# Expert jobs that write the finished token rows: one change to a graph layer with a mixture of experts

## The chip, the core and the metric

The kernel runs on one core of a Trainium2 chip. The metric is the device time of one execution in microseconds (us), taken without the profiler; the median of three runs of the kernel before is 1281.22 us (1278.25 to 1282.19). A core has five engines that matter here, each with its own instruction stream run in order: PE (TensorE, matrix products), DVE (VectorE, elementwise work), ACT (ScalarE), POOL (GpSimd; here it issues the indirect transfers), and SP (SyncE; here it issues the plain transfers). They wait for one another through semaphores.

## The reference

Two layers on 6,250 nodes of 256 numbers, with 100,000 edges sorted by destination:

```
x = x + gnn(layernorm(x), edges)      # attention over incoming edges, 4 heads of 64
x = x + ffn(layernorm(x))             # one of 8 experts for each node ("token")
```

The graph layer gathers, for each edge, two projections of its source node, mixes them by the edge's two factors, and sums them at the destination with softmax weights. In the expert layer each token goes to the expert with the highest gate probability:

```
idx   = argmax(probs);  prb = max(probs)
buf   = zeros(E, C, D).at[idx, pos].set(x)         # x is normalized here
ybuf  = relu(buf @ w1 + b1) @ w2 + b2              # 256 -> 1024 -> 256
y_tok = ybuf[idx, pos] * prb                       # and then added to the token's x2
```

Below, h is the normalized token, x2 the token before it (input plus graph layer), and prob its probability. The result of a token is y * prob + x2.

## The kernel before, in words

Preparation (the first 70 us) normalizes all nodes, projects them into a table in DRAM (`node_tab`), and turns the edge lists.

**Edge phase.** The edges come in 66 blocks of twelve tiles of 128 edges (`order`), from the highest destination down. For a block b, `gathers(b)` (L1045) issues on POOL one indirect transfer for each tile, into one of three buffers `gt`, three blocks ahead. `messages(b)` (L1053 on, DVE) mixes the rows, `places(b)` makes the one-hot matrix `hot`, `products(b)` the weighted messages `v`, and `windows(b, half)` sums them on PE (L1140); finished sums go from ACT to DRAM by SP (L1151). The main loop (L1505) writes this order out by hand; every engine's stream follows it, with `step_routing` and `step_experts` between the parts.

**Routing.** When the sums of a chunk of four token tiles are complete, `route` (L1161) loads them, forms x2 and h next to each other in one row `hx` of 514 numbers (h, x2, token number + 1, prob), picks the expert and the slot, and queues an indirect store of each tile's rows on POOL (`put`, L1259) into a buffer `bufs[p]` in DRAM. It also stores x2 alone in `x2_d` (L1190), except in the last pass.

**Passes.** Tokens are taken in four passes (LASTS, PASS): pass p gives each expert 256, 384, 256 and 128 slots. The slots are more than the tokens, so `bufs` are cleared first (`clear`, L922, from a tile of zeros; `clear_last`), a few clears in each of the early blocks. A pass's experts can start when all its tokens are put.

**Expert jobs.** `experts` (L1385) is a generator that yields after each piece with a cost; `step_experts` runs pieces up to a budget (SHARE) a block from block 13 on, so that PE has them between the edge sums. A job is one expert in one pass: `fetch_rows` (L1311) loads its slots, `columns` transposes h, then two products with `w1t` (L1409) and `w2t` (L1426), both loaded a job or two ahead on SP. `outputs` (L1341) comes one piece later: it adds the bias on DVE (L1346) and stores y to `ybufs[p]`. In the last pass `last_outputs` instead forms y * prob + x2 with `weighted` (L1372) from the row's second half, and `write_last` scatters the result to `out` from POOL.

**The last part.** After the edge loop (L1549) the edge buffers are given up for a third set of expert weights. While the remaining jobs run, `fetch_and_finish` (L1455) works off the tokens of the first three passes in pairs of tiles: `fetch_outputs` gathers their y from `ybufs` by an indirect transfer on POOL and loads x2 from `x2_d` on SP (L1446); `finish`, three pairs later, forms y * prob + x2 on DVE (`weighted`, L1374) and stores it to `out` on SP (L659). 22 pairs and 8 jobs of 128 slots are done this way. `weighted` also sums each row into a column of `finite`, by which a last check decides whether a slow general path has to run.

Of the kernel before, what the change touches and what calls it, by code (L numbers as in the profile page):

```python
# [8 lines left out]
F32 = mybir.dt.float32  # L9
# [5 lines left out]
P = 128  # L15
# [504 lines left out]
def kernel(  # L520
# [28 lines left out]
    nc = tc.nc  # L549
    N, D = x.shape  # L550
    NE = src.shape[0]
    _, H, O = attn.shape
    E, _, FF = w1.shape
# [5 lines left out]
    NT = -(-N // P)  # L559
# [32 lines left out]
    NP = len(PASS)  # L592
    SM = max(PASS)
    SLOTS = [E * S for S in PASS]
# [8 lines left out]
    dram = ctx.enter_context(tc.tile_pool(name="dram", bufs=1, space=bass.MemoryType.DRAM))  # L603
    node_tab = dram.tile([N, ROW], F32, name="node_tab")
    sums = dram.tile([TROWS, ACC], F32, name="sums")
    x2_d = dram.tile([NT * P, D], F32, name="x2_d")

    BW = 2 * D + 2

    bufs = [dram.tile([n + NT * P, BW], F32, name=f"buf{p}") for p, n in enumerate(SLOTS)]  # L610
# [3 lines left out]
    const = fast.enter_context(tc.tile_pool(name="const", bufs=1))  # L614
# [16 lines left out]
    nc.vector.memset(ones, 1.0)  # L631
    eps_t = const.tile([P, 1], F32, name="eps_t")
    nc.vector.memset(eps_t, EPS)
    zeros = const.tile([P, 1024], F32, name="zeros")
    nc.vector.memset(zeros, 0.0)

    no_edge = const.tile([P, 1], F32, name="no_edge")
# [28 lines left out]
    def moments(pool, t, k):  # L666

        st = pool.tile([P, k, nc.vector.BN_STATS_DIM], F32, name="ln_st")
        mv = pool.tile([P, k, nc.vector.BN_AGGR_DIM], F32, name="ln_mv")
        for n in range(k):  # L670
            nc.vector.bn_stats(st[:, n, :], t[:, n, :])
            nc.vector.bn_aggr(mv[:, n, :], st[:, n, :])
        sd = pool.tile([P, k], F32, name="ln_sd")
        nc.scalar.activation(sd, mv[:, :, 1], AF.Sqrt, bias=eps_t)
        return mv, sd
# [24 lines left out]
    with tc.tile_pool(name="p1", bufs=2) as p1, \  # L700
# [191 lines left out]
        for c in range(len(parts)):  # L892
# [8 lines left out]
            for n0 in range(0, len(parts[c]), 2):  # L901
                k = min(2, len(parts[c]) - n0)
# [18 lines left out]

    def clear(p, r):  # L922

        nc.sync.dma_start(bufs[p][r:r + 512, 0:D].rearrange("(p n) d -> p n d", n=4),
                          zeros.rearrange("p (n d) -> p n d", n=4))

    def clear_last():

        J = SLOTS[NP - 1] // P
        for j in range(0, J, 2):  # L930
            nc.sync.dma_start(bufs[NP - 1][j * P:(j + 2) * P, D:BW].rearrange("(p n) k -> p n k", n=2),
                              zeros[:, 0:2 * (D + 2)].rearrange("p (n k) -> p n k", k=D + 2))

    clears = [(p, r) for p in range(NP) for r in range(0, SLOTS[p], 512)]


    nc.sync.dma_start(sums[N:TROWS, :], zeros[0:TROWS - N, 0:ACC])
# [45 lines left out]
    prob = ep.tile([P, NT], F32, name="prob")  # L983
# [13 lines left out]
    with tc.tile_pool(name="p4", bufs=1) as p4, tc.tile_pool(name="p5", bufs=2) as p5, \  # L997
# [163 lines left out]
        def route(c, p):  # L1161


            tiles = chunks[c]
            k, n0 = len(tiles), tiles[0]
            n1, r0 = n0 + k, n0 * P
            hx = p4.tile([P, CK, BW], F32, name="hx", bufs=2)[:, :k, :]
            h, x2 = hx[:, :, 0:D], hx[:, :, D:2 * D]
# [17 lines left out]
            attn_out = part[:, :, 0:H * O].rearrange("p n (h o) -> p n h o", h=H)  # L1186
            nc.vector.tensor_mul(attn_out, attn_out, den.unsqueeze(3).to_broadcast([P, k, H, O]))
            nc.vector.tensor_add(x2, x2, part[:, :, 0:H * O])
            if p < NP - 1:
                nc.sync.dma_start(x2_d[r0:r0 + k * P, :].rearrange("(n p) d -> p n d", p=P), x2)  # L1190
            mv, sd = moments(p4, x2, k)
            yield 0.0
            normalized(p4, h, x2, mv, sd, k)
# [91 lines left out]
        w1s, w2s, xs, xm = {}, {}, {}, {}  # L1285
# [25 lines left out]
        def fetch_rows(i):  # L1311

            if i == taken["fetched"] and i < len(jobs) and jobs[i][0] < taken["rows"]:
                taken["fetched"] = i + 1
                p, e = jobs[i]
                S = PASS[p]
                J = S // P
                xs[i] = p5.tile([P, SM // P, D], F32, name="xe", bufs=3)[:, :J, :]
                rows = bufs[p][e * S:(e + 1) * S, :].rearrange("(p j) d -> p j d", j=J)
                nc.sync.dma_start(xs[i], rows[:, :, 0:D])  # L1320
                if p == NP - 1:
                    xm[i] = p6.tile([P, J, D + 2], F32, name="xm", bufs=E)
                    nc.sync.dma_start(xm[i], rows[:, :, D:BW])

# [16 lines left out]
        def outputs(py, i, j0, k):  # L1341
            p, e = jobs[i]
            S = PASS[p]
            J = S // P
            y = p5.tile([P, 2, D], F32, name="y")[:, :k, :]
            nc.vector.tensor_add(y, py, b2b[:, e, :].unsqueeze(1).to_broadcast([P, k, D]))  # L1346
            if p < NP - 1:
                nc.sync.dma_start(
                    ybufs[p][e * S:(e + 1) * S, :].rearrange("(p j) d -> p j d", j=J)[:, j0:j0 + k, :], y)
            else:  # L1350
                scatters.append((last_outputs(y, xm[i], e), xm[i]))
            if e == E - 1 and j0 + k == J and p < NP - 1:
                tiles = list(range(LASTS[p], LASTS[p - 1] if p else NT))
                due.extend((p, tiles[i:i + 2]) for i in range(0, len(tiles), 2))

        scatters, due = [], []
        finite = p4.tile([P, NT + SLOTS[NP - 1] // P], F32, name="finite")
        nc.vector.memset(finite, 0.0)

        def last_outputs(y, xe, e):  # L1360

            J = PASS[NP - 1] // P
            number, pr = xe[:, :, D], xe[:, :, D + 1]
            to = p6.tile([P, J], F32, name="to_f")
            nc.vector.tensor_scalar(to, number, 0.0, float(2 * N), op0=OP.is_equal, op1=OP.mult)
            row = p6.tile([P, J], I32, name="row_l", bufs=E)
            nc.vector.scalar_tensor_tensor(row, number, -1.0, to, op0=OP.add, op1=OP.add)
            for j in range(J):
                weighted(xe[:, j, 0:D], y[:, j, :], pr[:, j:j + 1], xe[:, j, 0:D], NT + e * J + j)
            return row  # L1370

        def weighted(to, y, w, x2, k):  # L1372

            nc.vector.scalar_tensor_tensor(to, y, w, x2, op0=OP.mult, op1=OP.add, accum_out=finite[:, k:k + 1])  # L1374
# [10 lines left out]
        def experts():  # L1385
# [6 lines left out]
            for i, (p, e) in enumerate(jobs):  # L1392
# [6 lines left out]
                for q in (i, i + 1):  # L1399
                    fetch_rows(q)  # L1400
# [33 lines left out]
        fetched = []  # L1434

        def fetch_outputs():

            p, tiles = due.pop(0)
            k, n0 = len(tiles), tiles[0]
            yg = p6.tile([P, 2, D], F32, name="yg", bufs=6)[:, :k, :]  # L1440
            for n in range(k):
                nc.gpsimd.indirect_dma_start(  # L1442
                    out=yg[:, n, :], out_offset=None, in_=ybufs[p],
                    in_offset=bass.IndirectOffsetOnAxis(ap=to_get[:, n0 + n:n0 + n + 1], axis=0))
            xr = p6.tile([P, 2, D], F32, name="xr", bufs=4)[:, :k, :]
            nc.sync.dma_start(xr, x2_d[n0 * P:(n0 + k) * P, :].rearrange("(n p) d -> p n d", p=P))  # L1446
            fetched.append((tiles, yg, xr))

        def finish():
            tiles, yg, xr = fetched.pop(0)  # L1450
            for n, t in enumerate(tiles):
                weighted(yg[:, n, :], yg[:, n, :], prob[:, t:t + 1], xr[:, n, :], t)
            store_nodes(out, yg, tiles)

        def fetch_and_finish(lag):  # L1455
# [47 lines left out]
        for b in range(3):  # L1503
            gathers(b)
        for b in range(NB + 1):  # L1505
            for clear_at in clears[2 * b - 2:2 * b] if b else ():
                clear(*clear_at)
            if b == E + 1:
                clear_last()
            if b < NB:  # L1510
                messages(b)
            step_routing()
            if b == NB - 2:

                last_chunk = routes_of(next_c)
                next_c += 1
                assert next_p == NP - 1
                next(last_chunk)
            if b == NB:
                routing.append(last_chunk)  # L1520
            if b:
                windows(b - 1, 0)
            step_experts(SHARE / 2)
            step_routing()
            if b < NB:
                places(b)
            step_routing()
            if b < NB:
                products(b)
            step_routing()  # L1530
            if b:
                windows(b - 1, 1)
            taken["released"] = taken["rows"]
            step_experts(SHARE / 2)
            while next_c < len(chunks) - 1 and done_at[next_c] < b:
                routing.append(routes_of(next_c))
                next_c += 1
            step_routing()
            pool_work.extend(todo)
            del todo[:]  # L1540
            if b + 3 < NB:
                gathers(b + 3)
            if wait_pass and not pool_work:
                taken["rows"] = wait_pass.pop() + 1
                i = (taken["rows"] - 1) * E
                if taken["jobs"] >= i - 1:
                    fetch_rows(i)
                    fetch_rows(i + 1)
        edge_pools.close()  # L1549
        p6 = last_pools.enter_context(tc.tile_pool(name="p6", bufs=2))  # L1550
# [102 lines left out]
```

## Time and profile before

| | |
|---|---|
| median of three runs | 1281.22 us |
| the profiled execution | 1762.93 us, span 1761.1 us |
| clock granted to PE in it, mean | 0.788 |
| POOL: edge gathers (L1045) | 782, 951 ns each |
| POOL: token gathers (L1442) | 44, 966 ns each |
| DVE: weighted sums (L1374) | 44 on tokens, 480 ns each; 8 in the last pass |
| SP: x2 stored (L1190), loaded (L1446) | 11 of 512 KB, 22 of 256 KB |
| SP: clears | 16 of 512 KB, 4 of 258 KB |
| SP: rows of a job (L1320) | 16 of 256 KB, 8 of 384 KB, 8 of 128 KB |
| bytes moved | 218.47 MB |

The profiled execution is much longer than the runs: it holds long stretches in which several engines stand still together. A line of groups gives line, engine, operation, tiles and count, then busy us and mean ns of one, then the idle time before them and what ended it. In order of time, a line is start, duration, engine and line, and in brackets the wait before it. Lines of waits give the total, the number and the longest, in us. "issue" is time in which the engine waited for nothing that the profile shows; "remote" or "an unknown queue" is a wait whose releaser the profile doesn't have.

### The profile page before, as it was taken

How to read it: one execution, taken by the hardware profiler on the slowest of the kernel's cores; microseconds unless marked ns; L12 is line 12 of the kernel's file. 1: busy time of each engine (PE TensorE's matmuls, PEld its weight loads, DVE VectorE, ACT ScalarE, POOL GpSimd, SP SyncE). 2: the span in 40 equal slices, each digit the busy share in tenths (PEclk: the TensorE clock that was granted, in tenths of full speed). 3: DMA queues.
4: the chain of work that ended last, by engine and by line, in shares of the span. 5: the costliest groups of instructions: out<-in, count | busy, mean ns of one | idle time of the engine just before them, and what ended most of it. 6: DMA issues, size and time to landing. Idle time of an engine off the chain costs nothing.

```text
span 1761.1 us, 14755 instructions
## 1 busy us (share of the span) xinstructions
PE 1110.9 (63%) x4658; PEld 893.4 (51%) x4658; DVE 870.6 (49%) x1879; ACT 282.0 (16%) x754; POOL 863.6 (49%) x912
## 2 busy tenths in 40 slices
PE   5531532544685656856577586476874787779875
PEld 5520422433574545745356365354653566568765
DVE  7652534756674544626247345543752446455322
ACT  3300100111220202112012111110201111111321
POOL 2577357256666162553653562734564563630443
PEclk9765767667887777868687796778886898879998
DMA  8233433345453434433443351433432344333893
GB/s 255 80 86 83 118 87 100 92 128 156 140 154 102 123 106 127 128 103 102 115 128 98 98 144 44 113 92 104 124 89 69 104 123 136 103 109 122 307 366 105
DMA packets 154149, 218.47 MB, mean 124 GB/s; under 512 B 20198, under 2 KB 125963, under 8 KB 153933
## 3 DMA queue, kind: packets, MB, share of 16 engines
q1 hardware_dynamic: 121981, 142.51, 25.4%
q0 software_dynamic: 31440, 73.83, 16.6%
q10 hardware_dynamic: 640, 1.09, 0.2%
q8 instruction: 39, 0.64, 0.2%
q14 instruction: 49, 0.40, 0.1%
HBM read 160.50 MB, written 57.25 MB: 124 GB/s over the span
## 4 chain that ended last, share of the span: by engine, by line
PE 41%; DVE 18%; another core or an unknown queue 17%; issue 15%; DMA 4%; POOL 3%; ACT 1%; SPq 0%; DVEq 0%; POOLq 0%; ACTq 0%
PE pv L1140 14%; PE py L1426 11%; PE ph L1409 9%; DVE v L1104 4%; POOL gt L1045 2%; DMA out_dram<-yg 2%; DVE hot L1088 2%; DVE m L1067 1%; DVE rv L1065 1%; PE pn L814 1%; PE pv L1139 1%; DVE gt L1060 1%; PE px L1335 1%; DMA gt<-node_tab,srci 1%
## 5 line engine op out<-in xcount | busy, mean ns | idle before, releaser
L1045 POOL DMA_INDIRECT gt<-node_tab,srci x782 | 743.7, 951 | 622.5 <-DVE sc L1070 390.0
L1140 PE MATMUL pv<-v,hot 128*128 128x260 f32 x1564 | 467.2, 443 | 217.3 <-issue 117.1
L1140 PEld LDWEIGHTS pv<-v,hot 128*128 128x128 f32 x1564 | 346.0, 225 | 303.1 <-issue 149.5
L1426 PE MATMUL py<-w2t,hf 128*128 128x256 f32 x1024 | 264.1, 408 | 121.7 <-issue 84.6
L1426 PEld LDWEIGHTS py<-w2t,hf 128*128 128x128 f32 x1024 | 207.0, 205 | 165.0 <-issue 96.7
L1409 PE MATMUL ph<-xT,w1t 128*128 128x256 f32 (+2 forms) x1024 | 252.6, 399 | 44.3 <-issue 43.2
L1409 PEld LDWEIGHTS ph<-xT,w1t 128*128 128x128 f32 x1024 | 184.8, 200 | 99.0 <-issue 55.3
L1088 DVE TENSOR_TENSOR hot<-fixed,local 128x1536 f32<-128x1536 f32 (+1 forms) x66 | 114.2, 1730 | 225.2 <-remote 225.2
L1104 DVE TENSOR_TENSOR v<-m,fixed 128x3072 f32<-128x3072 f32 (+1 forms) x66 | 218.7, 3314 | 2.3
L1412 ACT ACTIVATE hf<-ph,b1t 128x256 f32<-128x256 f32 (+2 forms) x256 | 107.2, 474 | 461.0 <-PE ph L1409 199.1
L1346 DVE TENSOR_TENSOR y<-py,b2b 128x512 f32<-128x512 f32 (+1 forms) x40 | 23.3, 582 | 250.5 <-PE py L1426 126.2
L1260 POOL DMA_INDIRECT buf<-hx,to_put x49 | 48.7, 993 | 100.4 <-DVE fixed L1058 50.0
L1442 POOL DMA_INDIRECT yg<-ybuf,to_get x44 | 42.5, 966 | 98.9 <-ACT part_b L1144 50.0
L1148 ACT COPY r<-pv 128x260 f32<-128x260 f32 x86 | 32.0, 372 | 314.4 <-remote 191.6
L1060 DVE TENSOR_TENSOR gt<-gt,fixed 128x816 f32<-128x816 f32 (+1 forms) x66 | 65.6, 993 | 32.4 <-DMA gt<-node_tab,srci 25.9
L1067 DVE TENSOR_TENSOR m<-gt,rv 128x408 f32<-128x408 f32 (+1 forms) x131 | 75.5, 576 | 4.5
L1065 DVE TENSOR_TENSOR rv<-gt,fixed 128x408 f32<-128x408 f32 (+1 forms) x131 | 76.1, 581 | 2.2
L1201 PE MATMUL pt<-ident,hx 128*128 128x128 f32 x98 | 21.8, 388 | 85.2 <-DVE hx L681 64.3
L1112 ACT COPY vl<-v 128x260 f32<-128x260 f32 x56 | 22.9, 408 | 257.3 <-issue 71.8
L1103 DVE COPY fixed<-v 128x48 f32<-128x48 f32 (+1 forms) x66 | 13.8, 209 | 99.7 <-ACT v L1080 95.8
L1201 PEld LDWEIGHTS pt<-ident,hx 128*128 128x128 f32 x98 | 16.8, 199 | 90.6 <-ACT r L1148 30.0
L1028 DVE TENSOR_REDUCE over_s<-pm 128x4 f32<-128x512 f32 x14 | 9.7, 690 | 106.2 <-PE pm L1016 51.8
(206 smaller groups left out, 825.5 us busy)
## 6 DMA issues: line engine op xcount, KB each, us to landing
w1t<-in_L_ffn_w_dram SPq DMA_DIRECT2D x30, 1024.0 KB
w2t<-in_L_ffn_w_dram SPq DMA_DIRECT2D x30, 1024.0 KB
gt<-node_tab,srci POOLq DMA_INDIRECT x782
sums<-r SPq DMA_DIRECT2D x86, 130.0 KB
buf<-zeros SPq DMA_DIRECT2D x16, 512.0 KB
part<-sums SPq DMA_DIRECT2D x12, 520.0 KB
ybuf<-y SPq DMA_DIRECT2D x24, 256.0 KB
x_d<-hx SPq DMA_DIRECT2D x11, 512.0 KB
```

What stands on the lines that cost most here:

```text
L1045: nc.gpsimd.indirect_dma_start(out=gts[b][:, i - i0, :], out_offset=None, in_=node_tab, in_offset=bass.IndirectOffsetOnAxis(ap=srci[:, i:i ...
L1060: nc.vector.tensor_mul(fw, fw, fac[:, 0, :n].unsqueeze(2).to_broadcast([P, n, MS]))
L1065: nc.vector.tensor_mul(rv[:, :k, :], gt[:, a0:a1, MS:ROW], fac[:, 1, a0:a1].unsqueeze(2).to_broadcast([P, k, MS]))
L1067: nc.vector.tensor_add(m[:, a0:a1, :], fw[:, a0:a1, :], rv[:, :k, :])
L1088: nc.vector.tensor_tensor(hot[:, :n, :], lane_p.unsqueeze(1).to_broadcast([P, n, P]), local[:, i0:i1].unsqueeze(2).to_broadcast([P, n, P]) ...
L1104: nc.vector.tensor_mul(v[:, :n, 0:H * O].rearrange("p n (h o) -> p n h o", h=H), m[:, :n, 0:O].unsqueeze(2).to_broadcast([P, n, H, O]), w[ ...
L1140: nc.tensor.matmul(pv, hot[:, i - i0, :], v[:, i - i0, :], start=(i == g0), stop=(i == g1 - 1))
L1260: ins = nc.gpsimd.indirect_dma_start(out=bufs[p], out_offset=bass.IndirectOffsetOnAxis(ap=to_put[:, n0 + n:n0 + n + 1], axis=0), in_=hx[:, ...
L1409: nc.tensor.matmul(ph[:, f - f0, :], w1t[:, d, f * P:(f + 1) * P], xT[:, d, :S], start=(d == 0), stop=(d == DC - 1))
L1412: nc.scalar.activation(hf[:, f, :S], ph[:, f - f0, :], AF.Relu, bias=b1t[:, e * FC + f:e * FC + f + 1])
L1426: nc.tensor.matmul(py[:, j - j0, :], hf[:, f, j * P:(j + 1) * P], w2t[:, f, :], start=(f == 0), stop=(f == FC - 1))
L1442: nc.gpsimd.indirect_dma_start(out=yg[:, n, :], out_offset=None, in_=ybufs[p], in_offset=bass.IndirectOffsetOnAxis(ap=to_get[:, n0 + n:n0 ...
```

## The change

The jobs of the first three passes do what those of the last pass did: they form y * prob + x2 from the row in their buffer, so that `ybufs` holds finished rows. `fetch_rows` loads the whole row of 514 numbers in one transfer in these passes; `outputs` calls `weighted` for each of its tiles; `fetch_outputs` only gathers, and `finish` only stores. `x2_d`, its stores and its loads are gone. Since the second half of a row is now read in every pass, whole rows are cleared: 32 clears of 256 rows, four in each of the early blocks, in place of 16 clears of the first halves of 512 rows and `clear_last`. The last pass is as before.

```diff
-    x2_d = dram.tile([NT * P, D], F32, name="x2_d")
...
-    zeros = const.tile([P, 1024], F32, name="zeros")
+    zeros = const.tile([P, 2 * (2 * D + 2)], F32, name="zeros")
...
-        nc.sync.dma_start(bufs[p][r:r + 512, 0:D].rearrange("(p n) d -> p n d", n=4),
-                          zeros.rearrange("p (n d) -> p n d", n=4))
-    def clear_last():
...
-    clears = [(p, r) for p in range(NP) for r in range(0, SLOTS[p], 512)]
+        nc.sync.dma_start(bufs[p][r:r + 256, :].rearrange("(p n) d -> p (n d)", n=2), zeros)
+    clears = [(p, r) for p in range(NP) for r in range(0, SLOTS[p], 256)]
...
-            if p < NP - 1:
-                nc.sync.dma_start(x2_d[r0:r0 + k * P, :].rearrange("(n p) d -> p n d", p=P), x2)
...
-                xs[i] = p5.tile([P, SM // P, D], F32, name="xe", bufs=3)[:, :J, :]
                 rows = bufs[p][e * S:(e + 1) * S, :].rearrange("(p j) d -> p j d", j=J)
-                nc.sync.dma_start(xs[i], rows[:, :, 0:D])
-                if p == NP - 1:
+                xe = p5.tile([P, SM // P, BW], F32, name="xe", bufs=3)[:, :J, :]
+                xs[i] = xe[:, :, 0:D]
+                if p < NP - 1:
+                    nc.sync.dma_start(xe, rows)
+                    xm[i] = xe[:, :, D:BW]
+                else:
+                    nc.sync.dma_start(xs[i], rows[:, :, 0:D])
                     xm[i] = p6.tile([P, J, D + 2], F32, name="xm", bufs=E)
                     nc.sync.dma_start(xm[i], rows[:, :, D:BW])
...
             if p < NP - 1:
+                for n in range(k):
+                    j = j0 + n
+                    weighted(y[:, n, :], y[:, n, :], xm[i][:, j, D + 1:D + 2], xm[i][:, j, 0:D],
+                             (sum(SLOTS[:p]) + e * S) // P + j)
                 nc.sync.dma_start(
                     ybufs[p][e * S:(e + 1) * S, :].rearrange("(p j) d -> p j d", j=J)[:, j0:j0 + k, :], y)
...
-        finite = p4.tile([P, NT + SLOTS[NP - 1] // P], F32, name="finite")
+        finite = p4.tile([P, sum(SLOTS) // P], F32, name="finite")
...
-            xr = p6.tile([P, 2, D], F32, name="xr", bufs=4)[:, :k, :]
-            nc.sync.dma_start(xr, x2_d[n0 * P:(n0 + k) * P, :].rearrange("(n p) d -> p n d", p=P))
-            fetched.append((tiles, yg, xr))
+            fetched.append((tiles, yg))
...
-            tiles, yg, xr = fetched.pop(0)
-            for n, t in enumerate(tiles):
-                weighted(yg[:, n, :], yg[:, n, :], prob[:, t:t + 1], xr[:, n, :], t)
+            tiles, yg = fetched.pop(0)
             store_nodes(out, yg, tiles)
...
-            for clear_at in clears[2 * b - 2:2 * b] if b else ():
+            for clear_at in clears[4 * b - 4:4 * b] if b else ():
                 clear(*clear_at)
-            if b == E + 1:
-                clear_last()
```

More of the change, by code (lines that the diff above doesn't have):

```diff
@@ L922, in clear @@
     def clear(p, r):
-        nc.sync.dma_start(bufs[p][r:r + 512, 0:D].rearrange("(p n) d -> p n d", n=4),
-                          zeros.rearrange("p (n d) -> p n d", n=4))
-    def clear_last():
[L929 to L932, printed above, removed]
-    clears = [(p, r) for p in range(NP) for r in range(0, SLOTS[p], 512)]
+        nc.sync.dma_start(bufs[p][r:r + 256, :].rearrange("(p n) d -> p (n d)", n=2), zeros)
+    clears = [(p, r) for p in range(NP) for r in range(0, SLOTS[p], 256)]
     nc.sync.dma_start(sums[N:TROWS, :], zeros[0:TROWS - N, 0:ACC])
@@ L1368, in last_outputs @@
             for j in range(J):
-                weighted(xe[:, j, 0:D], y[:, j, :], pr[:, j:j + 1], xe[:, j, 0:D], NT + e * J + j)
+                weighted(xe[:, j, 0:D], y[:, j, :], pr[:, j:j + 1], xe[:, j, 0:D],
+                         (sum(SLOTS[:-1])) // P + e * J + j)
             return row
```

## The prediction

> **What bounds the kernel now.** I read the page first (shares, groups), then POOL's waits and its instructions in order of time, then stretches of the last 110 us with the DMA rate, then the waits of those stretches. From the page:
>
> ```profile
> PE 1110.9 (63%) x4658; PEld 893.4 (51%) x4658; DVE 870.6 (49%) x1879; ACT 282.0 (16%) x754; POOL 863.6 (49%) x912
> ...
> L1045 POOL DMA_INDIRECT gt<-node_tab,srci x782 | 743.7, 951 | 622.5 <-DVE sc L1070 390.0
> ```
>
> No engine is full by these shares, but this execution took 1762.93 us (span 1761.1) against a median of 1281.22 unprofiled: some 480 us of it are not in the runs that count. The chain names them: 17.4% (306 us) of "another core or an unknown queue" and 15.0% (264 us) of issue, largely stalls of ten to thirty us in which several engines stand. So shares mislead, and I count work. POOL's waits up to the last edge gather:
>
> ```profile
> POOL gt L1045 <- DVE sc L1070: 390.0, 27, 28.2
> POOL gt L1045 <- issue: 231.7, 752, 2.7
> POOL buf L1260 <- DVE fixed L1058: 50.0, 6, 12.7
> POOL buf L1260 <- DVE late_by L1276: 29.1, 3, 13.1
> ```
>
> POOL, in order of time in an undisturbed early block:
>
> ```profile
> 112.85 0.95 POOL L1045 DMA_INDIRECT gt<-node_tab,srci  x1 [0.30 <-issue]
> 114.10 0.94 POOL L1045 DMA_INDIRECT gt<-node_tab,srci  x1 [0.30 <-issue]
> ```
>
> A gather starts every 1.25 us: twelve, a block, take 15.0 us. POOL gathers from 71.3 to 1578.4 us, 1507 us, less its waits for others (390 + 50 + 29 + 5 = 474): 1033 us. 71 + 1033 + 183 (from there to the end) = 1287, less the two stalls of 8.1 and 9.2 us in that last part = 1270. That is within 1% of 1281, so the unprofiled edge phase runs at POOL's pace. The other engines have room: two DVE blocks without a wait start at 1422.72 and 1432.63, 9.9 us apart, and early on DVE waits for gathers (24.0 us in four waits).
>
> The last part is another matter. Stretches (length, busy time of PE, its loads, DVE, ACT, POOL, clock, DMA share, GB/s), then the queues of the first stretch, and PE's waits from 1655 to 1735:
>
> ```profile
> 1655.00:1712.00 57.00, 44.75 (x279) 40.46 (x277) 16.61 (x80) 15.07 (x50) 19.85 (x21) 0.97 1.04 366
> 1712.00:1735.00 23.00, 16.85 (x102) 15.06 (x102) 5.35 (x26) 3.22 (x12) 15.22 (x16) 0.88 0.71 228
> ```
> ```profile
> DMA packets 15556, 20.88 MB, mean 366 GB/s; under 512 B 1047, under 2 KB 13526, under 8 KB 15553
> ...
> xr<-x_d SPq DMA_DIRECT2D x11, 256.0 KB
> ```
> ```profile
> PE px L1335 <- DMA xe<-buf: 8.5, 3, 4.5
> PE px L1335 <- remote: 2.4, 1, 2.4
> ```
>
> For 57 us the transfers are full at 366 GB/s, PE idles 12.2 of them, and it waits for rows that stand behind token loads and weights. This stretch is bound by bytes.
>
> **What the Trainium skill says.** "DMA: Bandwidth & Descriptors", section "Issuing engines are not separate DMA queues": transfers of all queues share the same 16 engines. The trace agrees: in the 57 us SP's queue takes 90.7% and the software queue 13.0%, together a full share. "SBUF — State Buffer", section "SBUF: two separate sides": a DVE instruction with two SBUF inputs and GpSimd can block one another, for the whole instruction; the page names descriptor writing as a victim for two-port modes, and for two inputs only GpSimd work that reads SBUF. Here two-input adds stretch gathers:
>
> ```profile
> 359.34 1.45 POOL L1045 DMA_INDIRECT gt<-node_tab,srci  x1 [0.30 <-issue]
> 360.01 1.23 DVE L1188 TENSOR_TENSOR hx<-hx,part 128x1024 f32<-128x1024 f32 x1
> ```
>
> A gather takes 0.947 us where no DVE work overlaps it, 1.45 here, 1.87 at worst. This matters, since the change brings such an instruction into POOL's phase.
>
> **The change, part by part.**
>
> (1) Token loads (xr) go: 22 of 256 KB. In the full stretch 11 start, and two more just before (1652.5, 1653.6) have their data in it. I count 12: 12 x 262 KB = 3.15 MB, at 366 GB/s 8.6 us. Bounds: all 22 (5.77 MB) in stretches that bind, 15.8 us; or nothing, if PE is held by something else next. After it the stretch needs 57 - 8.6 = 48.4 us for its bytes and PE 44.75, so bytes still bind and all 8.6 count. **-8.6.**
>
> (2) Token stores (x2_d, L1190, 11 of 512 KB) go: they lie in the edge phase at a third to a half of the DMA share. Taken as 0. SP stood 103.3 us for them waiting on DVE; cover being POOL's pace, a gain of 0 to 3.
>
> (3) 44 weighted sums of `finish` leave the last part. One starts every 0.41 us (0.48 busy, the next overlaps). DVE is mostly idle there (16.6 of 57 us); only the last two stand on the chain, 1749.10 to 1749.92: **-0.8**. The stores to `out` no longer wait for DVE, which stood behind PE (SP waited 33.2 us for yg); they wait for the gathers alone, issued three pairs earlier. This may bring weights forward: 0, gain up to 3.
>
> (4) 56 weighted sums (8 x 7 tiles) enter `outputs`: 56 x 0.41 = 23.0 us of DVE, nearly all in the edge phase. Behind them on DVE wait messages, hot and v of the next blocks; then PE's windows and, through gt's three buffers, POOL. The cover is POOL's 15.0 us a block against DVE's 9.9 (a routed chunk adds some 12 every four blocks, outputs 0.5): about 1.5 to 2 us spare on average, against 0.4 added. **0**; without cover 23. y's store leaves up to 0.82 us later, with SP's next entries; py is free before.
>
> (5) Port lock: y and the rows are both in SBUF. Where L1374 overlapped a gather in the last part (11 of them) it took 1.003 against 0.947 us: 0.056 each. POOL is at work 0.95/1.25 = 76% of the phase, so 43 of 56 meet one: **+2.4**. Bounds: 0, and 43 x 0.3 = 13 (half the stretch of the 1.23 us add).
>
> (6) Clears: 32 of 526 KB for 16 of 512 KB and 4 of 258 KB: 12 more issues on SP (0.6 us each, hidden) and 7.4 MB more written. Two took the DMA share to 0.84 from 98 to 103 us with some tail: about 4.6 us at full share for 1.05 MB. Four, in pieces of 4 KB instead of 1 KB, take 5.7 (at 366 GB/s) to 9.2 of a 15 us block that has 3 for gathers: they fit. Later gathers cost nothing while POOL has two blocks in hand; **0**, up to 5. The first clears stand at 24.1 us in a full stretch (331 GB/s): 1.05 MB more delay the x load at 30.45 by 3.2 us, and DVE wants it only after 44: 0, up to 2.
>
> (7) Row loads of 24 jobs double (7.3 MB more), in pieces of 4 to 6 KB instead of 1 KB, asked for a job ahead: 0; at three starts of a pass up to 1.5 each, so 4. `xe` is now read until the job's last output; its third buffer comes round after the first step of the next job, before the fetch that needs it: no wait. Wider `finite` and `zeros`: under 0.1.
>
> Sum: -8.6 - 0.8 + 2.4 = -7.0 us. Profiled execution: 1762.9 to 1756, in which stalls of either sign can drown it. The stretch and the end have the same work unprofiled, so I carry the microseconds, not the share, to the median: 1281.2 - 7.0 = **1274.2**.
>
> **Rivals.** A, the forecast: 1266 to 1279. B, the token loads are not what holds the last part, or the edge phase gives back the same: PE needs 44.75 us and takes over at once, or half of DVE's 23 us shows: -9.4 + 2.4 + 11.5 = +4.5, or -9.4 + 2.4 + 8.6 = +1.6: 1280 to 1286. For it: PE is busy 78% in the stretch; the profile doesn't show unprofiled slack. Against: its waits name the rows. C, slower: DVE's sums fall where they delay POOL, the in-order engine that sets the pace, by port lock or through late messages. All 56 at 0.41 us and the lock's 13: -9.4 + 23 + 13 = +26.6, 1308; half of both +8.6, 1290. It decides from a loss of 9.4 us on. For it: the stretches to 1.45 and 1.87 us. Against: 1.003 on average for just this instruction. D, more gain: all token loads counted, and SP freed: -15.8 - 0.8 + 2.4 - 5 = -19: 1262. For it: 335 GB/s is reached before 1643 too. Against: PE runs on there.
>
> **How the numbers follow.** A 0.55, B 0.15, C 0.18, D 0.12. 0.3%, 3.8 us, is about what a measurement of this kernel can tell from no change. Faster: D and most of A (0.50): 0.62. Same: the weak edge of A and most of B (0.10): 0.15. Slower: C and the rest of B: 0.23. The range takes D in whole and C to its middle, 1260 to 1291; A's own is 1266 to 1279.
>
> **What would show it.** Right: no xr in the last part; the full stretch 8 to 9 us shorter at the same GB/s; PE's waits for xe below 5 us; gathers still every 1.25 us; L1374's line with 56 sums in the edge phase. Wrong: gathers above 1.1 us beside sums (step 5), POOL waiting longer for sc in stretches without stalls (4), DVE waiting longer for gathers in blocks 1 to 8 (6), or PE idle in the last part as before (1).

## The result and the profile after

The changed kernel takes 1272.92 us (median of six runs, 1271.31 to 1276.78); the kernel before, on the same chip, 1280.07 us (1278.25 to 1283.55). The ratio is 0.995, 95% interval 0.9928 to 0.9972: 6.4 us faster by the ratio (3.6 to 9.2). 1274.2 was forecast.

The profile after is of an execution as long as the runs, 1272.38 us (span 1270.6). Executions fall into two groups, near 1280 and near 1770 us, and one and the same chip gave both (medians of the kernel before of 1279.33 and 1772.29 us in two comparisons), so the first profile (1762.93 us) and e2, e4, e5, e7, e9 and e12 below, of the long group, are compared only among themselves. The pages before and after must therefore not be set side by side in shares. The page after, engines and the groups of the edge gathers and of the sums' neighbour y:

```profile
PE 1007.3 (79%) x4658; PEld 846.7 (67%) x4658; DVE 878.6 (69%) x1903; ACT 281.6 (22%) x754; POOL 867.8 (68%) x912
...
L1036 POOL DMA_INDIRECT gt<-node_tab,srci x782 | 747.4, 956 | 244.2 <-issue 228.6
...
L1339 DVE TENSOR_TENSOR y<-py,b2b 128x512 f32<-128x512 f32 (+1 forms) x40 | 23.2, 581 | 93.4 <-PE py L1424 93.4
```

Its waits, POOL's and one of DVE's:

```profile
POOL gt L1036 <- issue: 228.6, 750, 0.3
DVE gt L1051 <- DMA gt<-node_tab,srci: 108.7, 26, 9.7
POOL buf L1249 <- DVE fixed L1049: 10.1, 3, 6.9
```

The 390 us for which POOL waited for DVE are not there. That is not the change's doing: e6, e8 and e11 below have the edge loop of before, and in their profiles, as long as the runs, this wait is 4.1, 8.9 and 4.5 us. The idle time before POOL's gathers is nearly all the 0.3 us between one and the next, and it is DVE that waits for gathers, 26 times. The gathers' first and last start are 1063.5 us apart, where the first profile, less its waits, gave 1033:

```profile
L1036 POOL DMA_INDIRECT gt<-node_tab,srci x782: 940/944/1957, 72.1 to 1135.6; - x196
```

For the last part, the same 75 us (1185 to 1260) of the changed kernel, engines first, then its transfers, then PE's waits:

```profile
1185.00:1260.00 75.00, 67.84 (x435) 62.05 (x433) 10.19 (x47) 21.67 (x74) 34.08 (x36) 0.98 0.86 298
```
```profile
DMA packets 15915, 22.37 MB, mean 298 GB/s; under 512 B 1414, under 2 KB 13402, under 8 KB 15910
```
```profile
PE px L1328 <- DMA xe<-buf: 5.8, 4, 2.9
```

The middle line is of the transfers (DMA). There is no load xr among them, the mean rate over the stretch is 298 GB/s and no longer full to its end (the share of the transfer engines is 0.86), and PE's waits for rows are 5.8 us.

### The profile page after: what moved, and what is told of

Its sections match the earlier page's. It is cut to its first block, busy times and chain, and to the rows that moved or that the text cites. A ratio compares the mean times of both kernels' runs of the same rounds, so it can differ in the third digit from the quotient of the medians.

```text
span 1270.6 us, 14749 instructions
## 1 busy us (share of the span) xinstructions
PE 1007.3 (79%) x4658; PEld 846.7 (67%) x4658; DVE 878.6 (69%) x1903; ACT 281.6 (22%) x754; POOL 867.8 (68%) x912
## 4 chain that ended last, share of the span: by engine, by line
PE 39%; POOL 22%; DVE 17%; issue 10%; DMA 8%; SPq 2%; ACT 1%; DVEq 0%; POOLq 0%; ACTq 0%
POOL gt L1036 20%; PE pv L1131 13%; PE py L1424 10%; PE ph L1407 9%; DVE v L1095 4%; DMA gt<-node_tab,srci 4%; PE pl L1198 2%; PE pn L813 2%; DMA xe<-buf 1%; POOL buf L1249 1%; PE pv L1130 1%; PE pt L1190 1%; DMA node_tab<-nt 1%; DVE m L1058 1%; DVE rv L1056 1%
## 5 line engine op out<-in xcount | busy, mean ns | idle before, releaser
L1036 POOL DMA_INDIRECT gt<-node_tab,srci x782 | 747.4, 956 | 244.2 <-issue 228.6
L1131 PE MATMUL pv<-v,hot 128*128 128x260 f32 x1564 | 427.2, 421 | 74.2 <-DVE v L1095 67.4
L1131 PEld LDWEIGHTS pv<-v,hot 128*128 128x128 f32 x1564 | 327.4, 213 | 138.8 <-issue 78.9
L1407 PE MATMUL ph<-xT,w1t 128*128 128x256 f32 (+2 forms) x1024 | 235.6, 383 | 0.7 <-ACT xT L1329 0.7
L1424 PE MATMUL py<-w2t,hf 128*128 128x256 f32 x1024 | 232.8, 381 | 0.5 <-ACT hf L1410 0.5
L1424 PEld LDWEIGHTS py<-w2t,hf 128*128 128x128 f32 x1024 | 193.1, 191 | 26.5 <-ACT hf L1410 0.9
L1407 PEld LDWEIGHTS ph<-xT,w1t 128*128 128x128 f32 x1024 | 177.3, 192 | 44.1 <-ACT xT L1329 1.1
L1071 ACT ACTIVATE v<-sc 128x48 f32<-128x48 f32 (+1 forms) x66 | 16.0, 242 | 315.0 <-DVE sc L1069 315.0
L1328 PE MATMUL px<-ident,xe 128*128 128x128 f32 x128 | 21.4, 281 | 27.1 <-DMA xe<-buf 27.1
```

Source lines behind the costliest of these rows:

```text
L1036: nc.gpsimd.indirect_dma_start(out=gts[b][:, i - i0, :], out_offset=None, in_=node_tab, in_offset=bass.IndirectOffsetOnAxis(ap=srci[:, i:i ...
L1131: nc.tensor.matmul(pv, hot[:, i - i0, :], v[:, i - i0, :], start=(i == g0), stop=(i == g1 - 1))
L1407: nc.tensor.matmul(ph[:, f - f0, :], w1t[:, d, f * P:(f + 1) * P], xT[:, d, :S], start=(d == 0), stop=(d == DC - 1))
L1424: nc.tensor.matmul(py[:, j - j0, :], hf[:, f, j * P:(j + 1) * P], w2t[:, f, :], start=(f == 0), stop=(f == FC - 1))
```

## Experiments

Differences to before are ratios of each comparison, less one, times 1280 us, with the 95% interval in brackets. A difference between two versions that were compared with before each in its own comparison has a half-width (half of its interval) worked out from theirs, added in squares. SBUF and PSUM, named below, are two memories of the core; PE writes its products to PSUM.

### The token loads put back (e1)

```diff
+            if p < NP - 1:
+                nc.sync.dma_start(x2_d[r0:r0 + k * P, :].rearrange("(n p) d -> p n d", p=P), x2)
...
+            xr = p6.tile([P, 2, D], F32, name="xr", bufs=3)[:, :k, :]
+            nc.sync.dma_start(xr, x2_d[n0 * P:(n0 + k) * P, :].rearrange("(n p) d -> p n d", p=P))
             fetched.append((tiles, yg))
```

> The changed kernel with the token rows x2 still stored by the routing and still loaded in the last part, though nothing reads them (three buffers in place of four, for space). Theory (the gain is the bytes of the token loads in a stretch where all transfers share a full bandwidth): the time goes back by about 8.6 us, to 1281 (1278 to 1283), and PE's waits for rows in the last part come back to about 11 us. Rival (the gain is that DVE and SP are no longer tied to one another in the last part, whatever is loaded): it stays at 1273, within 2 us.

Measured: 1284.74 us, ratio 1.0035 (1.0021 to 1.0049), +4.5 us to before and so 10.9 (7.6 to 14.2) to the changed kernel. This is above the expected 1278 to 1283. The same stretch, its transfers and PE's wait in this kernel:

```profile
1185.00:1260.00 75.00, 62.55 (x377) 56.66 (x376) 8.95 (x43) 18.83 (x64) 31.87 (x34) 0.91 1.02 356
```
```profile
DMA packets 20379, 26.73 MB, mean 356 GB/s; under 512 B 1589, under 2 KB 17873, under 8 KB 20375
...
xr<-x_d SPq DMA_DIRECT2D x15, 256.0 KB
```
```profile
PE px L1331 <- DMA xe<-buf: 12.4, 4, 4.4
```

The transfers are full for all 75 us, 4.36 MB more of them, 15 token loads among them (3.93 MB, 11.0 us at 356 GB/s), and PE works 5.3 us less. It also works more slowly: 377 products in 62.55 busy us at a granted clock of 0.91, against 435 in 67.84 at 0.98. Nothing reads what is loaded, so it is the transfers themselves, and with them full for the whole stretch their bytes are the likely reason. Their issue came back too, 22 times some 0.5 us on SP; the run doesn't part the two. The rival, that only the loosened coupling counts, falls.

### The loads alone taken from the kernel before (e6)

```diff
-            nc.sync.dma_start(xr, x2_d[n0 * P:(n0 + k) * P, :].rearrange("(n p) d -> p n d", p=P))
-            fetched.append((tiles, yg, xr))
+            fetched.append((tiles, yg, yg))
```

> The kernel before, without the token loads: each finished tile is summed with itself in place of x2, so the residual of the tokens of the first three passes is left out of the result; the stores of x2, the sums in the last part, the old clears and the half-row loads stay. Theory (bytes): 8 to 9 us faster than before, 1271.5. Rival (the loads are hidden, or PE is held by the next thing at once): within 2 us of before, 1280. If both the loads and the coupling through DVE count: about 5 us for this one alone.

Measured: 1271.61 us, ratio 0.9935 (0.9912 to 0.9957): -8.3 us (-11.3 to -5.5). In the 75 us:

```profile
1185.00:1260.00 75.00, 65.03 (x421) 59.80 (x419) 24.33 (x114) 20.37 (x71) 33.07 (x34) 0.95 0.81 283
```

As the theory had it, from the other side: the loads alone give as much as the whole change does, with the old sums still in the last part.

### Only the sums taken from the last part (e8)

```diff
-            for n, t in enumerate(tiles):
-                weighted(yg[:, n, :], yg[:, n, :], prob[:, t:t + 1], xr[:, n, :], t)
```

> The kernel before with its token loads, but with no weighted sums in the last part: gathered rows go straight to the output, so the probability and the residual are left out for the tokens of the first three passes. Theory (bytes): only the two sums on the final chain are saved, about 0.8 us: 1279. Rival (the coupling of SP's stores to DVE, which stands behind PE, held back the weights): 4 us or more, 1276 or less.

Measured: 1278.72 us, ratio 0.9985 (0.9969 to 1.0): -1.9 us (-4.0 to 0). 0.8 lies in it; a coupling worth 4 us or more is at its edge. PE still waits about as long for rows in the 75 us as in e1 (and in e11, which has the sums and the loads, 9.5 us):

```profile
PE px L1335 <- DMA xe<-buf: 11.2, 4, 4.8
```

So with the loads in place it doesn't help PE that SP's stores are free of DVE.

Where the time lies is seen from the last gather's start to the end of the span, one profile each:

| kernel | token loads | last gather, us | from there to the end, us |
|---|---|---|---|
| e8, no sums in the last part | yes | 1138.5 | 143.4 |
| e1, change with loads | yes | 1136.0 | 146.7 |
| e11, before with the new clears | yes | 1129.6 | 147.8 |
| changed kernel | no | 1135.6 | 135.0 |
| e3, sums from PSUM | no | 1134.3 | 134.3 |
| e10, change without sums | no | 1133.2 | 135.3 |
| e6, before without loads | no | 1130.5 | 136.2 |

With the loads the last part takes 143 to 148 us, without them 134 to 136, whatever else is changed: the means differ by 10.8 us. Only a part of it is PE standing idle. From the last gather to the last expert's end PE has about the same work in all of them. In e1 it is idle 13.9 of 134.5 us there and busy 120.6 at a mean granted clock of 0.95, in the changed kernel idle 9.4 of 123.0 and busy 113.6 at 0.99; e8 and e6 differ the same way, by 5.5 idle and 2.7 busy. In the edge phase single profiles differ too much for a few us: e6 and e8 have the same program up to there and are 8 us apart.

### The weighted sums read PSUM (e3)

```diff
-            nc.vector.tensor_add(y, py, b2b[:, e, :].unsqueeze(1).to_broadcast([P, k, D]))
+            to = py if p < NP - 1 else y
+            nc.vector.tensor_add(to, py, b2b[:, e, :].unsqueeze(1).to_broadcast([P, k, D]))
...
-                    weighted(y[:, n, :], y[:, n, :], xm[i][:, j, D + 1:D + 2], xm[i][:, j, 0:D],
+                    weighted(y[:, n, :], py[:, n, :], xm[i][:, j, D + 1:D + 2], xm[i][:, j, 0:D],
```

> The changed kernel with the bias added in PSUM and the weighted sum read from there, so that the 56 sums have one input in SBUF and one in PSUM in place of two in SBUF. Theory (the only cost of the sums in the edge phase is the port that DVE and GpSimd share, 2.5 us by the trace): 2 to 3 us faster than the changed kernel, 1270.5. Rival (no such cost, or the same with PSUM): 1273, within 1 us.

Measured: 1273.73 us, ratio 0.9949 (0.9934 to 0.9964), no difference to the changed kernel that can be told (0.1 us, 3.4 either way). The effect on POOL is there all the same. In the changed kernel, in order of time, a sum and a gather beside it:

```profile
959.68 0.48 DVE L1372 SCALAR_TENSOR_TENSOR y<-y,xe 128x256 f32<-128x256 f32 x1
959.80 1.18 POOL L1036 DMA_INDIRECT gt<-node_tab,srci  x1 [0.30 <-issue]
```

In e3, a gather that starts as long after the start of a sum:

```profile
953.57 0.48 DVE L1373 SCALAR_TENSOR_TENSOR y<-py,xe 128x256 f32<-128x256 f32 x1
953.70 0.94 POOL L1036 DMA_INDIRECT gt<-node_tab,srci  x1 [0.31 <-issue]
```

In the changed kernel 32 gathers and 7 puts overlap a sum; they take 0.997 and 1.104 us in the mean, against 0.945 and 0.990 of those beside neither a sum nor the routing's two large instructions: 2.5 us in all. Only 12 of the 39 are longer, those that start inside a sum. In e3, 34 and 7 overlap one and take 0.950 and 0.988. So it is the two SBUF inputs of the sum that lengthen gathers, and one in PSUM ends it. But POOL waited 26.3 us for DVE in e3 where it waited 22.2 in the changed kernel (one profile each, 0.3 us gaps put down to DVE included): what POOL gains it may wait for elsewhere. The run can't tell 2 us from none. Another cost of e3 is not excluded: its PSUM tile `py` stays in use until the sums have read it.

### The clears alone (e4, e11)

```diff
+        nc.sync.dma_start(bufs[p][r:r + 256, :].rearrange("(p n) d -> p (n d)", n=2), zeros)
...
-            for clear_at in clears[2 * b - 2:2 * b] if b else ():
+            for clear_at in clears[4 * b - 4:4 * b] if b else ():
```

> The kernel before with the clears of the change alone (32 of whole rows, four in each early block). The changed kernel with its loads put back came out 4 us above the kernel before, so some part of the change costs in the edge phase. If it is the clears: 3 to 6 us slower than before, 1284 to 1286, with later landings of gathers in blocks 1 to 8. If they are hidden, as predicted: within 1.5 us of before, 1280.

Measured: 1774.58 us against 1772.29 of before, ratio 1.0009 (0.998 to 1.0037), which tells nothing of 3 us. Again:

> The same kernel as the one before with the clears of the change alone, again, for the same reason. On a chip where before takes 1280: 3 to 6 us slower than before if the clears are what costs in the edge phase (ratio 1.002 to 1.005), within 1.5 us if they are hidden. On a chip of the other kind: no change that can be told, since POOL isn't the pace there.

Measured: 1282.54 us against 1279.33, ratio 1.0026 (1.0016 to 1.0036): +3.3 us (2.0 to 4.6). The clears are not free. Where they cost isn't shown: in this profile POOL's gathers run from 71.2 to 1129.6 us, 1058.4, no longer than in e6 (1059.2), which has the old clears. DVE's wait for gathers from 70 to 260 us is 64.6 us against 63.1. The profiled execution, 1279.1 us, is the shortest of the 22 of this kernel, so the 3.3 us need not be in it.

### The sums left out of the jobs (e2, e10)

```diff
             if p < NP - 1:
-                for n in range(k):
-                    j = j0 + n
-                    weighted(y[:, n, :], y[:, n, :], xm[i][:, j, D + 1:D + 2], xm[i][:, j, 0:D],
-                             (sum(SLOTS[:p]) + e * S) // P + j)
```

> The changed kernel without the 56 weighted sums in the jobs: y is stored as it comes from the bias add, so probability and residual are left out for the tokens of the first three passes; row loads, clears and the last part are those of the change. Theory (POOL's pace covers DVE's 23 us; only the shared port costs): 0 to 3 us faster than the changed kernel, 1270 to 1273. Rival (DVE is not covered): 8 to 23 us faster, 1265 or less.

Measured: 1760.53 us against 1772.29 of before, ratio 0.9924 (0.9879 to 0.9968). Again:

> The same kernel as the changed one without its 56 sums, again, since the last comparison fell on a chip on which the kernel before takes 1772 us. On a chip where before takes 1280: the changed kernel with its loads put back was 4 us above the kernel before; if the sums are what costs in the edge phase, this one is 4 to 6 us faster than the changed kernel, 1267 to 1269 (ratio to before 0.990 to 0.992); if they are covered, it is within 2 us of it, 1271 to 1274 (0.993 to 0.996). On a chip of the other kind: some 13 us faster than before once more, of which the changed kernel itself, not run there, would have some 7 to 10.

Measured: 1267.45 us (four runs), ratio 0.9897 (0.9877 to 0.9916), -13.2 us to before and 6.8 (3 to 10.6) better than the changed kernel. By the middle of the interval the 23 us of sums cost less than a third of their own length. Where, the profiles show only in part. POOL's gathers in the changed kernel and in e10:

```profile
L1036 POOL DMA_INDIRECT gt<-node_tab,srci x782 | 747.4, 956 | 244.2 <-issue 228.6 <-DVE sc L1061 4.6 <-DMA gt<-node_tab,srci 4.6
L1036 POOL DMA_INDIRECT gt<-node_tab,srci x782 | 744.4, 952 | 244.2 <-issue 228.9 <-DMA gt<-node_tab,srci 4.9 <-DVE sc L1061 4.0
```

With the sums the gathers themselves take 3.0 us longer, and POOL's idle time before them is the same 244.2 us. A wait of POOL for a later DVE would stand there, and doesn't. But e10's profiled execution, 1270.22 us, is the longest of its four, 2.2 us short of the changed kernel's 1272.38; the rest of the 6.8 is in neither profile.

A second estimate comes from e1, which differs from before by the sums and the whole rows in the jobs, the clears, and the sums gone from the last part: 4.5 + 1.9 - 3.3 = 3.1 us (0.1 to 6.1) for sums and rows, if the parts add.

### The sums twice (e7)

```diff
-                for n in range(k):
+                for n in list(range(k)) + list(range(k)):
```

> The changed kernel with each of the 56 weighted sums done twice in a row (the second adds the same again, so the result differs): 23 us more of DVE in the edge phase. Theory (covered): 0 to 3 us slower than the changed kernel, 1273 to 1276. Rival (DVE is not covered): 10 us or more, 1283 and up.

Measured: 1767.82 us against 1772.29 of before, ratio 0.9998 (0.9961 to 1.0034). Against e2, beside it, two rounds of sums (46 us of DVE) cost 0.74% by the ratios (0.17 to 1.31), some 13 us of 1772, but 7.3 us by the medians. It says nothing of the kernel at 1280 us, where POOL sets the pace.

### Two versions meant to beat both (e9, e12)

e9 also sends the routing's product to PSUM, in halves of two tiles; e12 is e9 with two clears in a block.

```diff
-            nc.vector.tensor_mul(attn_out, attn_out, den.unsqueeze(3).to_broadcast([P, k, H, O]))
-            nc.vector.tensor_add(x2, x2, part[:, :, 0:H * O])
+            for n in range(0, k, 2):
+                kk = min(2, k - n)
+                pa = ps2.tile([P, 2, D], F32, name="pa", tag="acc", bufs=4)[:, :kk, :]
+                nc.vector.tensor_mul(pa.rearrange("p n (h o) -> p n h o", h=H), attn_out[:, n:n + kk],
+                                     den[:, n:n + kk, :].unsqueeze(3).to_broadcast([P, kk, H, O]))
+                nc.vector.tensor_add(x2[:, n:n + kk, :], x2[:, n:n + kk, :], pa)
...
-            for clear_at in clears[4 * b - 4:4 * b] if b else ():
+            for clear_at in clears[2 * b - 2:2 * b] if b else ():
```

> The changed kernel with both kinds of sums with two SBUF inputs out of the way of GpSimd: the weighted sums read PSUM, and the routing's product of sums and reciprocals goes to PSUM in halves of two tiles, from where it is added to x2. The trace of the changed kernel has 6.5 us of gathers stretched beside that addition and 2.5 beside the weighted sums. If what stretches a gather moves the end: 5 to 9 us faster than the changed kernel, 1264 to 1268. If POOL's time is made up elsewhere: within 2 us of it, 1273.

> A version to beat both: the changed kernel with the weighted sums and the routing's addition reading PSUM, and with two clears of whole rows in a block instead of four, over sixteen blocks instead of eight. If the clears' 3.3 us come from their density and the stretched gathers' 9 us count: 1262 to 1267. If only the clears count: 1269 to 1271. If neither: 1273, and on the slow kind of chip no difference from the changed kernel that can be told.

Measured: e9 1774.47 us against 1772.29 of before, ratio 1.0023 (0.9991 to 1.0055), and e12 1787.34 against 1780.92, ratio 1.0027 (0.9996 to 1.0058). They beat nothing. Whether they would where POOL sets the pace was not measured. Nor does their edit do all that was meant: the product `pa` still reads two SBUF inputs, and all four gathers in each profile that start well inside it still end 0.81 us after it (the last section has more on this).

### The kernel before, once more (e5)

> The kernel before, unchanged, for a profile on a chip where it takes 1280 us, if this call falls on one. There POOL's gathers should run from 71 to about 1133 us with a few us of waits, as in the profile of the changed kernel, and transfers in the last part should be full for some 70 us against 53 there. On the other kind of chip it should show the waits of the first profile again.

Measured: one run of 1758.14 us; 27 other runs of the same kernel beside it have a median of 1780.92. So the kernel before has no profile at 1280 us. Its waits:

```profile
POOL gt L1045 <- DVE sc L1070: 383.7, 27, 23.6
POOL gt L1045 <- issue: 231.6, 752, 2.7
```

They are those of the first profile. Since the 27 others are as long, the long waits are no work of the profiler.

## Why the prediction was right, step by step

**What bounds the kernel.** Right for the runs that count: POOL's pace and a last part bound by bytes are both seen in the profile after. The sum that confirmed it, 1270 against 1281, was close by luck. Its edge phase, 1033 us, is some 26 short of the 1059.2 between the first and last gather of e6, which has the edge loop of before, and its last part, 183 - 17 = 166 us, is some 20 longer than the 143 to 148 of the kernels with loads. The 480 us that I set aside are real where they occur (e5); there POOL waits 383.7 us for DVE, and POOL doesn't set the pace.

**Step 1, token loads, -8.6.** Right: -8.3 alone (e6), 10.9 when put back with the stores (e1). The count was low: in e1 15 loads start in the 75 us in which the transfers are full, not 12 in 57 us. Its sign, PE's waits for rows below 5 us, was just missed, with 5.8. And not all of the gain is waits: with the loads PE is also busy longer for about the same work, at a lower granted clock, which the step doesn't have.

**Step 2, stores of x2, 0.** Not tried alone. e1 against e6 leaves 2.6 us for stores and what else differs, 4.4 either way.

**Step 3, sums leaving the last part, -0.8.** -1.9 (-4.0 to 0) in e8: in keeping.

**Steps 4 and 5, sums in the edge phase, 0 and +2.4.** Together they measured +6.8 (3 to 10.6) by e10, and with the rows +3.1 (0.1 to 6.1) by way of e1: more than forecast, or as much. Step 5 was right in its total, 2.5 us by the trace, but not in its working: 12 transfers are held, by some 0.2 us each, and not 43 lengthened by 0.056. Its sign of being wrong came up: six gathers beside sums take over 1.1 us, up to 1.20. It also named the wrong instruction in the first profile. The gather at 359.34 us was under way before the addition L1188 began; it started inside the multiplication before that:

```profile
358.75 1.23 DVE L1187 TENSOR_TENSOR part<-part,den 128x1024 f32<-128x1024 f32 x1
```

Step 4, the cover, stays open. For it speaks that POOL's idle time is the same with and without the sums, 244.2 us. Against it speaks that e3, which ends the holding and keeps DVE's 23 us, gains nothing, while e10 is 6.7 us (3.5 to 9.8) better than e3. The sums done twice (e7) would have tested it where POOL sets the pace, but took 1767.82 us. That DVE's time is what costs is argued and not shown.

**Step 6, clears, 0.** Wrong in size and inside its bound of 5: +3.3 (2.0 to 4.6).

**Step 7** was not tried alone.

**The sum** came out right, -7.0 against -6.4, in part by luck. The parts measured alone give -8.3 - 1.9 + 3.3 + 6.8 = -0.1; the whole measured -6.4. Since the 6.8 was itself taken against the changed kernel, the gap of 6.3 is that between the first three parts, -6.9, and e10's -13.2, and their half-widths (2.9, 2.0, 1.3 and 2.5 in squares) allow 4.5. So more was gained than the parts tried alone account for, and it made up for what the sums and clears cost above the forecast. It may be the stores of x2, or the parts' working on one another. That stays open.

**The rivals.** B's first half, that PE takes over at once, falls with e1 and e6. Its second half, that half of DVE's sums show (11.5 us), is more than either estimate allows. C had its mechanism, sums that cost in the edge phase, at 6.8 us by the larger estimate, short of the 9.4 from which it decides. D did not come.

## What to carry to other kernels

Read a byte-bound stretch apart from the rest: what leaves it is worth about its bytes over the measured rate (here 3.93 MB at 356 GB/s, 11.0 us, against 8.3 and 10.9 measured), and it can be tested by putting the same bytes back unread. Work moved under cover need not be free to the last us: leaving 23 us of such DVE work out gained 6.8 us (3 to 10.6), of which the trace shows 2.5. Add the parts that were measured alone, and see whether they give the whole; here they don't. And from a profile longer than the runs take the sums of work, which were good here (743.7 us of gathers against 747.4), and not the shares and waits.

## What the runs showed that I had not expected

In the first profile PE starts single products 0.7 to 2.1 us apart from 1443 to 1459 us, each 0.4 to 0.6 us long, and the time between them is put down to issue; why is not shown. The mean granted clock of PE is 0.788 in that profile and 0.784 in e5, against 0.897 in the changed kernel's, and waits of POOL for DVE that make up 384 to 390 us there are 4.6 us here.

DVE instructions with two inputs in SBUF hold POOL's indirect transfers, and the traces show when: it depends on how the transfer starts, not on how long the two overlap. In the changed kernel 24 transfers start more than 0.08 us after the beginning of such an instruction (the sums, and the routing's multiplication L1178) and more than 0.13 before its end; all end 0.81 to 0.87 us after it, where an undisturbed gather takes 0.944 in all. In e1 21 of 23 do; the other two start less than 0.10 us into a sum. So the multiplication of 1.23 us makes a gather of up to 1.96:

```profile
772.80 1.23 DVE L1178 TENSOR_TENSOR part<-part,den 128x1024 f32<-128x1024 f32 x1
772.88 1.96 POOL L1036 DMA_INDIRECT gt<-node_tab,srci  x1 [0.30 <-issue]
774.06 1.23 DVE L1179 TENSOR_TENSOR hx<-hx,part 128x1024 f32<-128x1024 f32 x1
```

The addition L1179, which begins while this gather runs, adds nothing to it. Nor do the large products of the edge phase, one input of which (`fixed`) is in PSUM, though the 3.3 us of `v` run beside 208 gathers, 0.945 us in the mean:

```profile
962.19 3.35 DVE L1095 TENSOR_TENSOR v<-m,fixed 128x3072 f32<-128x3072 f32 x1
962.54 0.94 POOL L1036 DMA_INDIRECT gt<-node_tab,srci  x1 [0.30 <-issue]
```

The expectation of e9 put the 6.5 us of longer gathers beside the routing down to its addition; by these traces they belong to the multiplication.
